# Where the softmax weights of a banded attention are masked: one mask on VectorE and a difference on GpSimd, or GpSimd and TensorE for early tiles and VectorE alone for late ones

## The chip, the cores and the metric

The kernel runs on one core of a Trainium2 chip. The metric is the device time of one execution in microseconds (us). The kernel before was run four times: 921.56, 920.98, 919.06 and 921.23 us, a median of 921.1 us. Five engines work side by side, each through its own instructions in order: TensorE (PE, with its weight loads as PEld), VectorE (DVE), ScalarE (ACT), GpSimd (POOL) and SyncE (SP), which issues most DMAs. They wait for one another through semaphores.

## The reference, cut to what matters

A batch of four sequences, `x` of shape (4, 1024, 128), goes through four residual blocks: `x + attention(layernorm(x))`, `x + ffn(layernorm(x))`, `x + mamba(layernorm(x))`, and the ffn again. The change lies in the attention alone:

```python
sliding = causal & (cols >= rows - WINDOW + 1)        # WINDOW = 32
strided = causal & ((rows - cols) % STRIDE == 0)      # STRIDE = 64
scores = jnp.where(sliding | strided, einsum('bhqd,bhkd->bhqk', Q, K) * HEAD_DIM ** -0.5, -jnp.inf)
out = einsum('bhqk,bhkd->bhqd', softmax(scores), V)   # 16 heads of 8
```

So a query sees the last 32 positions, itself among them, and every 64th position before it.

## The kernel before, in words

**Tiles.** The attention (lines 201 to 590) works on 32 tiles of 128 queries. A tile is 64 positions of two sequences at once (`bp` is the pair of sequences, `m` the tile's place among the 16 of its pair). I call tiles 0 to 15, of the first pair, pass 0, and tiles 16 to 31 pass 1. In a tile the 128 queries are four groups of 32. The window of a query reaches over two such groups, its own and the one before, and the two parts never meet: for each place k from 0 to 31 in a group a query at place q takes the own group's key if k <= q, and the key of the group before if k > q. So the kernel holds one matrix of 32 scores for each query and head, in which `copy_predicated` (lines 395 to 404) chooses by `prev_mask` between the two. The strided part, `m` more scores for each head, comes from elementwise products (`prod`, line 386) on GpSimd, which VectorE sums.

**Steps of one tile.** `scores`: TensorE (PSUM tile `ps`), ScalarE copies into `S` (line 379). `product`: GpSimd makes `prod`, 128 x 128m elements. `scores_before`: VectorE's `copy_predicated`. `softmax_scores`: VectorE sums `prod`, takes the maximum `mx` and subtracts it. `softmax_exp`: ScalarE makes `E`. `strided_products`: GpSimd makes `prodv` of `E` and the strided values, 128 x 128m elements; `strided`: VectorE sums it into `or`. `weights`: TensorE turns `E`'s 512 window weights over (PSUM tile `pt`, keys on the partitions). Then the weights are parted, which is what the change touches (lines 462 to 475): `weights_own` (VectorE) multiplies `pt` by the mask `own_t` into `eo`; `weights_all` (ScalarE) copies `pt` into `ep`; `weights_before` (GpSimd) subtracts, `ep = ep - eo`. `values` (lines 486 to 512): TensorE adds up in the PSUM tile `pa` the strided sums, 16 products of `eo` with the own group's values, and 16 (8 for m = 0) of `ep` with the values of the group before; four of these small matmuls stand side by side on the array. `divide`: VectorE divides by the sum of weights (`rden`, `o`). `turn_out`, `keep_out`, `project_out`, `residual`: TensorE turns `o` over, ScalarE keeps it (`oT`), TensorE multiplies by `woT` (`py`), VectorE adds to `x`.

**What sets the order.** The loop of lines 546 to 590 writes the order out by hand. Each engine call goes through `InOrder` (lines 49 to 62, hence L57 for nearly every instruction of the profile), which keeps it in the order of the program on its engine. In one turn i the steps belong to different tiles: GpSimd has `prodv(i-1)`, `prod(i+1)`, then the subtraction for tile i-2; VectorE `copy_predicated(i)`, `divide(i-4)`, `strided(i-2)`, the mask for i-2, `residual(i-5)`, the softmax of i; ScalarE the copy `ep(i-2)`, the copy `S(i+1)`, the exponential `E(i)`, and after it `oT(i-4)` and the copies that belong to projections of later tiles (`prep_steps`, lines 274 to 348) and `vb`; TensorE the turn of E(i-2), `py(i-5)`, `scores(i+1)`, projections, `turn_out(i-4)` and `values(i-3)`. Layer norm statistics of the ffn (`st_fa`, `mv_fa`, `rs_fa`) are put between these by the scheduler.

**Buffers.** `prod` and `prodv` share three buffers, so that `prod(i+1)` waits until VectorE has read `prodv(i-2)`. `eo`, `ep` and `kT` have two each. `kT` holds keys of four tiles on their way, by 16 DMAs, into the tile `kx`.

**What follows.** The ffn and the Mamba block (a scan over time, lines 1059 to 1154), interleaved by pieces with due times (lines 1157 to 1207), take the rest of the span. Their first instructions wait until the attention's buffers are given back.

Of the kernel before, what the change touches and what calls it, by code (L numbers as in the profile page):

```python
# [16 lines left out]
F32 = mybir.dt.float32  # L17
# [4 lines left out]
AF = mybir.ActivationFunctionType  # L22
ALU = mybir.AluOpType
# [3 lines left out]
P = 128  # L27
# [5 lines left out]
W = 32  # L33
# [6 lines left out]
CH = 512  # L40
# [3 lines left out]
def hybrid_kernel(ctx: ExitStack, tc: tile.TileContext, x, Wq, Wk, Wv, Wo, ln_g, ln_b, W_in, conv_w,  # L44
# [17 lines left out]
    ve, te, sc, gp = (InOrder(e) for e in (nc.vector, nc.tensor, nc.scalar, nc.gpsimd))  # L62
# [19 lines left out]
    for bp in range(NP):  # L82
        t = xpool.tile([P, NT, C], F32, tag=f"x{bp}", name=f"x{bp}")
# [13 lines left out]
    own_t = const.tile([P, W], F32, name="own_t")  # L97
    prev_t = const.tile([P, W], F32, name="prev_t")
# [102 lines left out]
    def attention(actx):  # L201
# [5 lines left out]
        ap2 = actx.enter_context(tc.tile_pool(name="att2", bufs=2))  # L207
# [3 lines left out]
        tiles = [(bp, m) for bp in range(NP) for m in range(NT)]  # L211
# [9 lines left out]
        VQ = W + 4  # L221
# [52 lines left out]
        def prep_steps(cc):  # L274

            bp, c = divmod(cc, NT // 4)
            yield
            xn = ap2.tile([P, 4, C], F32, name=f"xn{cc}", tag="xn")
            rs = norms.pop(cc)
            for i in range(4):  # L280
                sc.activation(
                    xn[:, i, :], xs[bp][:, 4 * c + i, :], AF.Identity, bias=rs[:, 1, i : i + 1],
                    scale=rs[:, 0, i : i + 1],
                )
            yield
            tp = spare(f"tp{cc}")
            for i in range(4):
                te.transpose(tp[:, i * P : (i + 1) * P], xn[:, i, :], ident)
            yield
            xnT = ap2.tile([P, CH], F32, name=f"xnT{cc}", tag="xnT")  # L290
            sc.copy(xnT, tp)
            yield
            pq, pk = spare(f"pq{cc}"), spare(f"pk{cc}")
            te.matmul(pk, wqkv[:, 1, :], xnT, start=True, stop=True)
            te.matmul(pq, wqkv[:, 0, :], xnT, start=True, stop=True)

            def project(i):
                pn = spare(f"pn{cc}_{i}")
                te.matmul(
                    pn[:, : 3 * C], xnT[:, i * P : (i + 1) * P], wqkv.rearrange("p i c -> p (i c)"),  # L300
                    start=True, stop=True,
                )
                return pn

            qs = ap2.tile([P, 4, C], F32, name=f"qs{cc}", tag="qs")

            def keep_rows(i, pn):
                m = 4 * c + i
                sc.copy(qs[:, i], pn[:, :C])
                sc.copy(kv[bp][:, m], pn[:, C : 3 * C])  # L310
                sc.copy(vS[bp][:, :, m], pn[:, 2 * C : 3 * C])

            yield
            kx = kxs[cc % 2]
            qT = ap2.tile([P, CH], F32, name=f"qT{cc}", tag="qT")
            if cc == 0:

                sc.copy(qT, pq)
                for t in range(4):
                    ve.tensor_tensor(  # L320
                        kx[:, t], pk[:, t * P : (t + 1) * P].unsqueeze(1).to_broadcast([P, HB, P]),
                        head_of.unsqueeze(2).to_broadcast([P, HB, P]), ALU.mult,
                    )
            else:
                kT = ap2.tile([P, CH], F32, name=f"kT{cc}", tag="kT")
                sc.copy(kT, pk)
                queues = (nc.sync, nc.gpsimd) if cc == 1 else (nc.sync,)
                for h in range(H):
                    rows = slice(h * HD, (h + 1) * HD)
                    queues[h % len(queues)].dma_start(  # L330
                        kx[rows, :, h % HB, :], kT[rows, :].rearrange("p (t x) -> p t x", t=4)
                    )
                sc.copy(qT, pq)
            prep[cc] = qT, kx
            for i0 in (0, 2):
                yield
                pn = project(i0), project(i0 + 1)
                yield
                keep_rows(i0, pn[0])
                keep_rows(i0 + 1, pn[1])  # L340
            vd = dram.tile([4, P, C], F32, name=f"vd{cc}")
            nc.sync.dma_start(vd.rearrange("t p c -> p t c"), kv[bp][:, 4 * c : 4 * c + 4, C:])
            vr = ap2.tile([P, 16, C], F32, name=f"vr{cc}", tag="vr")
            for a in range(4):
                nc.sync.dma_start(
                    vr[a * W : (a + 1) * W], vd.rearrange("t (g k) c -> k (t g) c", k=W)
                )
            prep[cc] = qT, kx, qs, vr


        S, E, prods, prodv, ew, psum, outs = ({} for _ in range(7))
# [103 lines left out]
        def weights(i):  # L455
# [3 lines left out]
            for j in range(4):  # L459
                te.transpose(pt[:, j * P : (j + 1) * P], e[:, j * P : (j + 1) * P], ident)  # L460

        def weights_own(i):
            eo = ap2.tile([P, 16, W], F32, name=f"eo{i}", tag="eo")
            pt3 = psum["t", i].rearrange("p (a q) -> p a q", q=W)
            ve.tensor_tensor(eo, pt3, own_t.unsqueeze(1).to_broadcast([P, 16, W]), ALU.mult)
            ep = ap2.tile([P, 16, W], F32, name=f"ep{i}", tag="ep")
            ew[i] = eo, ep

        def weights_all(i):
            sc.copy(ew[i][1].rearrange("p a q -> p (a q)"), psum.pop(("t", i)))  # L470

        def weights_before(i):

            eo, ep = ew[i]
            gp.tensor_sub(ep, ep, eo)

        def spread_values(cc, heads):
            vr = prep[cc][3]
# [7 lines left out]
        def values(i):  # L486

            bp, m = tiles[i]
            eo, ep = (t.rearrange("p (j g) q -> p j g q", g=4) for t in ew.pop(i))

            def value(g, j):
                k, g = divmod(4 * i + g, 16)
                return vbs[k % 2][:, g, j]

            pa = spare(f"pa{i}")[:, : 4 * VQ]
            psum["a", i] = pa.rearrange("p (j c) -> p j c", j=4)
            te.matmul(
                pa, ident, outs.pop(i).rearrange("p j c -> p (j c)"), start=True, stop=False, skip_group_check=True
            )
            for j in range(4):  # L500
                for g in range(4):
                    te.matmul(
                        pa[g * W : (g + 1) * W, j * VQ : (j + 1) * VQ], eo[:, j, g], value(g, j),
                        start=False, stop=False, skip_group_check=True,
                    )
            for j in range(4):
                for g in range(4):
                    if g % 2 or m:
                        te.matmul(
                            pa[g * W : (g + 1) * W, j * VQ : (j + 1) * VQ], ep[:, j, g], value(g - 1 if g % 2 else g - 3, j),  # L510
                            start=False, stop=j == 3, skip_group_check=True,
                        )
        def divide(i):
            pa = psum.pop(("a", i))
            rden = small.tile([P, 4, 4], F32, name=f"rden{i}", tag="rden", bufs=2)
# [30 lines left out]
        for i in range(-LEAD, last + 5):  # L546
            def at(k, stage):
                if 0 <= i + k < last:
                    stage(i + k)

            if i == -LEAD:
                weights_in()
            if i == 0:
                load_mlp()
            at(-1, strided_products)
            at(1, product)
            at(-2, weights)
            at(0, scores_before)
            at(-4, divide)
            at(-2, strided)  # L560
            at(-2, weights_own)
            at(-2, weights_all)
            at(-2, weights_before)
            at(-5, project_out)
            at(-5, residual)
            if i == 3 - LEAD:
                scores(0)
                keep_scores(0)
            if i >= 0:
                at(1, scores)  # L570
                at(1, keep_scores)
            at(0, softmax_scores)
            at(0, softmax_exp)
            if i in starts:
                preps.append(prep_steps(starts[i]))
            for p in preps:
                next(p, None)
            at(-4, turn_out)
            at(-3, values)
            at(-4, keep_out)  # L580
            for p in preps:
                next(p, None)
            cc, step = divmod(i + LEAD, 4)
            if cc + 2 < last // 4:
                stats(cc + 2, range(step, step + 1))
                if step == 3:
                    scales(cc + 2)
            cc, step = divmod(i + 1, 4)
            if 0 <= cc < last // 4:
                spread_values(cc, range(step, step + 1))  # L590
# [714 lines left out]
```

## Time and profile before

| what | us |
|---|---|
| median of four runs | 921.1 |
| the profiled execution | 921.56 |
| its span, first to last instruction | 919.8 |
| first DVE instruction of turn 5 | 46.35 |
| of turn 16 (first of pass 1) | 127.34 |
| of turn 31 | 221.69 |
| last DVE addition into x of the attention ends | 246.09 |
| busy in the span: PE, DVE, POOL, ACT | 756.4, 756.6, 746.6, 593.0 |
| DVE mask `eo`, one of 32 | 0.68 |
| ACT copy `ep`, one of 32 | 0.59 |
| POOL subtraction `ep`, one of 32 | 1.28 |

How it is read: all times are of one execution, counted from its first instruction. "Busy" is the time in which an engine executes; a matmul's end is modelled. Instructions of one engine overlap a little: where two stand back to back, the second starts some 0.08 us (DVE) before the first is shown to end, so a step on DVE is taken from start to start. The profile names tiles without their numbers; which turn a row belongs to follows from its size (`prod` of tile m has 128m elements for each partition).

### The profile page before, as it was taken

The numbers are of one execution on the slowest core, as the hardware profiler recorded it, in microseconds if no ns is written. First come the engines' busy times: TensorE is split into PE (matmuls) and PEld (weight loads), VectorE is DVE, ScalarE is ACT, GpSimd is POOL, SyncE is SP. The second block draws the span as 40 slices with busy tenths as digits, with TensorE's granted clock in tenths as the row PEclk, the third lists the DMA queues.
The fourth block names the chain that finished last, engine by engine and source line by source line (L and its number), as shares of the span: only waits on it lengthen the run. The fifth ranks groups of instructions, "written<-read, shape, count | busy, mean of one in ns | idle before, by whom it ended". The sixth has DMA issues, their size and how long they took to land.

```text
span 919.8 us, 15260 instructions
## 1 busy us (share of the span) xinstructions
PE 756.4 (82%) x5642; PEld 454.2 (49%) x5642; DVE 756.6 (82%) x1014; ACT 593.0 (64%) x1299; POOL 746.6 (81%) x580
## 2 busy tenths in 40 slices
PE   5897678865797979797789878979989889788897
PEld 2454345543476534442356434425455446455567
DVE  6799898999633278989699978897999999999862
ACT  4776447743445487789856777887777865654523
POOL 6799996999523189899988988999989999989730
PEclk9899869996599979897999997977999899899899
DMA  5633213330100111112111111212122211122001
GB/s 133 121 72 68 57 22 68 73 65 2 42 7 1 47 61 56 46 69 71 51 66 68 47 69 48 68 48 68 51 80 66 81 70 61 66 81 80 24 1 35
DMA packets 47162, 53.09 MB, mean 58 GB/s; under 512 B 4824, under 2 KB 38400, under 8 KB 47088
## 3 DMA queue, kind: packets, MB, share of 16 engines
q1 hardware_dynamic: 45920, 51.59, 19.7%
q8 instruction: 44, 0.72, 0.3%
q0 software_dynamic: 608, 0.27, 0.2%
q10 hardware_dynamic: 560, 0.26, 0.1%
q14 instruction: 30, 0.25, 0.1%
HBM read 45.82 MB, written 4.46 MB: 55 GB/s over the span
## 4 chain that ended last, share of the span: by engine, by line
DVE 22%; PE 21%; POOL 11%; ACT 9%; issue 5%; DVEq 0%; POOLq 0%; ACTq 0%
DVE hs L57 14%; POOL db L57 5%; DVE hc L57 5%; PE pys L57 4%; PE pga L57 3%; POOL hc L57 3%; PE pc L57 3%; ACT da L57 3%; ACT L57 2%; PE pgb L57 2%; PE pgc L57 1%; POOL rs_z L57 1%; ACT waste L57 1%; PE pd L57 1%; PE pfob L57 1%
## 5 line engine op out<-in xcount | busy, mean ns | idle before, releaser
L57 POOL TENSOR_TENSOR db<-du,bs 128x1024 f32<-128x1024 f32 x128 | 302.7, 2366 | 0.9 <-DMA bs<-bd 0.9
L57 ACT ACTIVATE da<-dt,a_t 128x512 f32<-128x512 f32 x256 | 175.9, 689 | 126.6 <-DVE hs L57 126.1
L57 POOL TENSOR_TENSOR hc<-hc,hc 128x512 f32<-128x512 f32 x128 | 163.1, 1275 | 44.4 <-DVE hc L57 44.2
L57 DVE TENSOR_TENSOR hc<-hs,pcc 128x1024 f32<-128x1024 f32 x128 | 156.0, 1219 | 30.2 <-PE pcc L57 22.5
L57 DVE TENSOR_TENSOR_SCAN hs<-da,db 128x512 f32<-128x512 f32 x128 | 149.3, 1206 | 15.9 <-ACT da L57 15.7
L57 DVE TENSOR_TENSOR_SCAN hs<-da,carry,db 128x512 f32<-128x512 f32 x128 | 157.0, 1267 | 4.5 <-ACT da L57 4.5
L57 PE MATMUL pys<-hc,ident 128*128 128x512 f32 x256 | 147.1, 661 | 0.8 <-POOL hc L57 0.8
L57 PE MATMUL pcc<-bc,spread 96*128 96x512 bf16 x128 | 52.3, 408 | 35.8 <-DVE hc L57 34.9
L57 PE MATMUL pga<-h1a,w 128*128 128x512 f32 x256 | 76.8, 452 | 3.8 <-ACT gate L57 1.8
L57 PEld LDWEIGHTS pys<-hc,ident 128*128 128x128 f32 x256 | 51.3, 210 | 51.6 <-issue 32.1
L57 POOL TENSOR_TENSOR prodv<-vS,E 128x128 f32<-128x128 f32 (+14 forms) x30 | 69.4, 2315 | 5.5 <-ACT E L57 5.3
L57 POOL TENSOR_TENSOR prod<-kv,qs 128x128 f32<-128x128 f32 (+14 forms) x30 | 71.1, 2370 | 1.5 <-DVE or L57 1.4
L57 PEld LDWEIGHTS pga<-h1a,w 128*128 128x128 f32 x256 | 52.9, 210 | 29.9 <-issue 7.9
L57 PE MATMUL pc<-mxnT,w_conv 128*128 128x512 f32 x128 | 61.8, 609 | 5.9 <-ACT gate L57 5.9
L57 ACT ACT_TABLE_LOAD x48 | 61.6, 1283 | 3.5 <-issue 2.6
L57 PE MATMUL pgb<-h1b,w 128*128 128x512 f32 x192 | 59.0, 453 | 4.4 <-DVE fxnTc L57 3.1
L57 ACT ACTIVATE E<-S 128x512 f32<-128x512 f32 (+15 forms) x62 | 26.5, 474 | 52.2 <-DVE S L57 52.0
L57 PEld LDWEIGHTS pgb<-h1b,w 128*128 128x128 f32 x192 | 38.2, 200 | 26.6 <-issue 7.4
L57 PE MATMUL ps<-kx,qT 64*32 64x256 f32 x1008 | 46.0, 434 | 6.2 <-DVE S L57 5.3
L57 PE MATMUL py<-woT,oT 128*128 128x128 f32 x64 | 18.0, 368 | 39.7 <-ACT oT L57 38.4
L57 POOL TENSOR_TENSOR ep<-ep,eo 128x512 f32<-128x512 f32 x32 | 41.0, 1281 | 10.0 <-ACT ep L57 8.7
L57 ACT COPY ep<-pt 128x512 f32<-128x512 f32 x32 | 18.8, 587 | 38.4 <-DVE eo L57 35.8
(223 smaller groups left out, 1551.5 us busy)
## 6 DMA issues: line engine op xcount, KB each, us to landing
bs<-bd SPq DMA_DIRECT2D x64, 512.0 KB
vr<-vd SPq DMA_DIRECT2D x32, 256.0 KB
vd<-kv SPq DMA_DIRECT2D x8, 256.0 KB
x<-in_L_attn_a_x_dram SPq DMA_DIRECT2D x15, 128.0 KB
kx<-kT SPq DMA_DIRECT2D x104, 16.0 KB
out_dram<-x SPq DMA_DIRECT2D x12, 128.0 KB
taps<-in_L_attn_b_conv_w_dram SPq DMA_DIRECT2D x1, 512.0 KB
k1s<-in_L_ffn_k_dram SPq DMA_DIRECT2D x1, 256.0 KB
```

The source lines that it names most:

```text
L57: ins = getattr(self.engine, name)(*args, **kwargs)
```

## The change

Tiles with m >= 12 are "late", four in each pass; the other 24 are early.

For an early tile VectorE does nothing here any more. ScalarE copies `pt` into `ep` as before, and `ep` stays as it is: all weights. GpSimd makes `eo` by multiplying `ep` by `own_t`. One turn later ScalarE makes a new tile `el = -eo`. `values` adds 16 (8) matmuls for `el` beside those for `ep`: the sums over the group before are those of all weights less those of the own ones. For a late tile VectorE multiplies `pt` by `own_t` into `eo` and by `prev_t` into `ep`; ScalarE and GpSimd do nothing. `el` has one buffer, and `kT` has one in place of two.

```diff
-                kT = ap2.tile([P, CH], F32, name=f"kT{cc}", tag="kT")
+                kT = ap2.tile([P, CH], F32, name=f"kT{cc}", tag="kT", bufs=1)
...
+        def late_tile(i):
+            return tiles[i][1] >= 12
+
+        def masked(engine, dst, src, mask):
+            engine.tensor_tensor(dst, src, mask.unsqueeze(1).to_broadcast([P, 16, W]), ALU.mult)
+
         def weights_own(i):
-            eo = ap2.tile([P, 16, W], F32, name=f"eo{i}", tag="eo")
-            pt3 = psum["t", i].rearrange("p (a q) -> p a q", q=W)
-            ve.tensor_tensor(eo, pt3, own_t.unsqueeze(1).to_broadcast([P, 16, W]), ALU.mult)
-            ep = ap2.tile([P, 16, W], F32, name=f"ep{i}", tag="ep")
-            ew[i] = eo, ep
+            ew[i] = [ap2.tile([P, 16, W], F32, name=f"{n}{i}", tag=n) for n in ("eo", "ep")]
+            if late_tile(i):
+                pt3 = psum.pop(("t", i)).rearrange("p (a q) -> p a q", q=W)
+                masked(ve, ew[i][0], pt3, own_t)
+                masked(ve, ew[i][1], pt3, prev_t)
 
         def weights_all(i):
-            sc.copy(ew[i][1].rearrange("p a q -> p (a q)"), psum.pop(("t", i)))
-
-        def weights_before(i):
-            eo, ep = ew[i]
-            gp.tensor_sub(ep, ep, eo)
+            if not late_tile(i):
+                sc.copy(ew[i][1].rearrange("p a q -> p (a q)"), psum.pop(("t", i)))
+
+        def weights_apart(i):
+            if not late_tile(i):
+                masked(gp, *ew[i], own_t)
+
+        def weights_less(i):
+            if not late_tile(i):
+                less = ap2.tile([P, 16, W], F32, name=f"el{i}", tag="el", bufs=1)
+                sc.activation(less, ew[i][0], AF.Copy, scale=-1.0)
+                ew[i].append(less)
...
-            eo, ep = (t.rearrange("p (j g) q -> p j g q", g=4) for t in ew.pop(i))
+            eo, *before = (t.rearrange("p (j g) q -> p j g q", g=4) for t in ew.pop(i))
...
-            for j in range(4):
-                for g in range(4):
-                    if g % 2 or m:
-                        te.matmul(... ep[:, j, g], value(g - 1 if g % 2 else g - 3, j) ...)
+            for e in before:
+                for j in range(4):
+                    for g in range(4):
+                        if g % 2 or m:
+                            te.matmul(... e[:, j, g], value(g - 1 if g % 2 else g - 3, j) ...)
...
             at(-2, strided)
+            at(-3, weights_less)
             at(-2, weights_own)
             at(-2, weights_all)
-            at(-2, weights_before)
+            at(-2, weights_apart)
```

In the built program the order of all other instructions is the same on all five engines, in the attention and behind it.

More of the change, by code (lines that the diff above doesn't have):

```diff
@@ L505, in values @@
                     )
-            for j in range(4):
-                for g in range(4):
-                    if g % 2 or m:
[L509 to L512, printed above, removed]
+            for e in before:
+                for j in range(4):
+                    for g in range(4):
+                        if g % 2 or m:
+                            te.matmul(
+                                pa[g * W : (g + 1) * W, j * VQ : (j + 1) * VQ], e[:, j, g],
+                                value(g - 1 if g % 2 else g - 3, j), start=False, stop=j == 3, skip_group_check=True,
+                            )
         def divide(i):
```

## The prediction

> **What bounds the kernel now.** I first looked at the page's busy lines: DVE and PE 82%, POOL 81%, no engine alone. The change touches the attention only, so I asked for the engines' busy time in its stretches (the columns: stretch, its length, busy us of PE, PEld, DVE, ACT and POOL with counts, granted PE clock, DMA):
>
> ```profile
> 46.35:69.51 23.16, 20.56 (x442) 13.12 (x440) 22.89 (x58) 16.20 (x44) 21.75 (x16) 1.00 0.37 72
> 69.51:105.55 36.04, 27.33 (x545) 17.49 (x545) 35.70 (x72) 20.54 (x56) 35.07 (x27) 0.91 0.25 51
> 105.55:135.93 30.38, 19.00 (x251) 11.13 (x251) 25.25 (x45) 12.46 (x32) 28.93 (x14) 0.68 0.26 49
> 135.93:163.19 27.26, 24.86 (x579) 16.30 (x581) 23.87 (x58) 19.72 (x54) 19.95 (x28) 0.98 0.31 62
> 163.19:226.40 63.21, 44.27 (x1039) 29.38 (x1028) 61.22 (x98) 33.60 (x84) 62.30 (x28) 0.89 0.25 49
> 226.40:246.10 19.70, 11.90 (x252) 9.20 (x252) 13.19 (x22) 3.42 (x10) 12.91 (x8) 0.59 0.01 2
> ```
>
> Turns 5 to 8 (first row) are paced by DVE: 22.89 of 23.16. From turn 9 on DVE and POOL are both full, and in 105.55:135.93 POOL alone (28.93 of 30.38, DVE 25.25). The timeline says which of two full engines decides. GpSimd, at the start of its unbroken run:
>
> ```profile
> 61.99 1.29 POOL L57 TENSOR_TENSOR ep<-ep,eo 128x512 f32<-128x512 f32 x1
> 63.85 2.07 POOL L57 TENSOR_TENSOR prodv<-vS,E 128x896 f32<-128x896 f32 x1 [0.57 <-ACT E L57]
> 65.89 2.64 POOL L57 TENSOR_TENSOR prod<-kv,qs 128x1152 f32<-128x1152 f32 x1
> 68.48 1.27 POOL L57 TENSOR_TENSOR ep<-ep,eo 128x512 f32<-128x512 f32 x1
> ```
>
> and VectorE where it has caught up with GpSimd:
>
> ```profile
> 109.90 1.75 DVE L57 TENSOR_REDUCE or<-prodv 128x128 f32<-128x1536 f32 x1 [3.16 <-POOL prodv L57]
> ...
> 113.83 2.02 DVE L57 TENSOR_REDUCE S<-prod 128x224 f32<-128x1792 f32 x1 [1.13 <-POOL prod L57]
> ...
> 122.83 2.16 DVE L57 TENSOR_REDUCE S<-prod 128x240 f32<-128x1920 f32 x1 [0.60 <-POOL prod L57]
> ```
>
> The bracket is the idle time before the row and who ended it. After 63.85 GpSimd waits for nobody until 133.5; in pass 1, from 165 on, it idles 0.5 us before 168.41 and 0.24 before 175.38, then never until 237.9. GpSimd's work grows by some 0.55 us a tile (two products of 128m elements), VectorE's by 0.33, so every pass turns from VectorE's into GpSimd's. A third row matters at the end, ScalarE's copy and GpSimd's subtraction behind VectorE's mask:
>
> ```profile
> 239.89 0.59 ACT L57 COPY ep<-pt 128x512 f32<-128x512 f32 x1 [4.65 <-DVE eo L57]
> ```
>
> ```profile
> 236.64 1.30 POOL L57 TENSOR_TENSOR ep<-ep,eo 128x512 f32<-128x512 f32 x1
> 240.56 1.27 POOL L57 TENSOR_TENSOR ep<-ep,eo 128x512 f32<-128x512 f32 x1 [2.62 <-ACT ep L57]
> ```
>
> **Prices.** VectorE's mask shows 0.68 us, but the next instruction starts 0.59 to 0.60 later (65.39 to 65.98): I take 0.6, taken from 24 tiles and added to 8. GpSimd's subtraction is 1.28. A GpSimd multiply by a repeated mask isn't in the trace. The rows of its size are prod 128x512 at 1.28, prodv 128x512 at 1.07, and prodv 128x640 at 1.68, which is 1.34 for 512. I take 1.28, since in prod too one operand is repeated over the outer dimension; 1.07 and 1.34 are kept for the range. So early tiles change nothing on GpSimd, late ones free it of 1.28 each. ScalarE's el is nearest to E 128x512 (0.63, SBUF to SBUF) and the copy ep (0.59); queued back to back such copies start 0.48 apart: 0.5, within 0.48 to 0.63. TensorE's 16 more matmuls: ep's follow eo's by 0.29 (62.26 to 62.55), 0.49 at half clock; 24 times 0.3 is 7 us on an engine with 3 us and more idle per 20.
>
> el could force ScalarE to change function tables. The trace shows no table load from 25 to 247, although Identity, Exp and plain copies alternate there; a scaled Copy activation isn't among them. The Trainium skill, "ScalarE: Activation LUTs", section on table sets, says that cheap functions like copy lie in every set, so no load would come. If loads came all the same, two of 1.28 (the profile's ACT_TABLE_LOAD row, mean 1283 ns) for each of 24 tiles would put 62 us on ScalarE; since Identity and plain copies need none beside Exp, I leave this out of the cases.
>
> kT with one buffer costs nothing: the projection that feeds the next kT stands on TensorE behind the scores that wait for all of the former kT's DMAs.
>
> **The sum, in order of time** (turn i starts with copy_predicated of tile i).
>
> 1. *Turns 2 to 8.* Up to turn 4 ScalarE paces (it is full), and el only replaces its waits: 0. Then VectorE gains 0.6 a turn. But GpSimd idles only 0.28 (before 56.47), 0.15 (57.90) and 0.57 (63.85) there, and 0.52 before 46.52, of which I count 0.2; so its front comes forward by 1.2 us at most; its next work, prodv of tile 7, would start at 62.65 instead of 63.85. Gain 1.2; VectorE's other savings turn into waits for prod.
> 2. *Turns 9 to 13.* GpSimd paces, same work: 0.
> 3. *Turns 14 to 17.* GpSimd loses 4 x 1.28, VectorE gets 4 x 0.6. prod of tile 14 is still 1.2 early. From there VectorE, no longer waiting (its 0.60 before 122.83 goes), paces with 9.1 us a turn: turn 16 starts 1.1 early, turn 18 only 0.7. So late tiles give back 0.5 here.
> 4. *Turns 17 to 22.* Around 142.8 to 148.4 ScalarE is the limit (5.42 busy of 5.62; VectorE waits 1.68 for its copy S). In turn 17 it has no ep to copy, in turn 18 no el yet: the 0.7 stays. From turn 19 VectorE gains 0.6 a turn, ScalarE pays 0.5, and turn 21, with 5.50 busy of 5.67, gives some of it back. I get E of tile 22 and its prodv 1.0 early.
> 5. *Turns 23 to 31.* GpSimd's last idle (0.24) goes too: 1.25. Then it paces up to prod of tile 31, now ending at 226.37: 0 more.
> 6. *Tail.* The two subtractions at 226.37 and 231.38 are gone. prodv of tile 30 follows at once (225.1); that of tile 31 has to wait for its E, whose softmax starts at prod's end: 225.1 + 4.2 to the last subtraction + 0.9 for E = 230.2, ends 234.35 instead of 236.7. VectorE then sums it (2.4) and masks twice (1.2): 237.95. Before, the last weights were ready at 241.83 (mask to 239.8, copy to 240.5, subtraction); now TensorE is bound by po of tile 30 at 238.8, one turn of matmuls before the last rden: 240.9 against 243.38. Gain of the attention's end: 2.5.
>
> Behind it all instructions keep their order and wait for the attention's buffers, so 2.5 us should go through. The profiled execution took 921.56, 1.76 more than its span: 921.56 - 2.5 = 919.1. It was the slowest of four runs, 0.46 above their median; on the median of 921.1 this is **918.6 us**.
>
> The rest is not perfectly rigid: the granted clock is 0.59 in 226.40:246.10, and the four runs spread over 2.5 us. The Trainium skill, "TensorE: Matmul & The Clock Gate", in "What's actually happening", says the gate follows activity in free-running windows of about 3.4 us. By that page a shift of 2.5 us may land the ffn's first matmuls in another window, an estimate of up to 1.7 us either way.
>
> **Rivals.**
>
> *A cheaper mask.* With GpSimd at 1.07, the 13 masks in its paced stretches (tiles 6 to 11 and 21 to 27) save another 2.7: 915.9. Only one size of prodv speaks for it. At 1.34 they cost 0.8: 919.4.
>
> *The gain is given back.* VectorE's second mask falls in four turns where it is nearly as full as GpSimd (in 163.19:226.40 it is 61.22 of 63.21). If steps 1 and 4 bring nothing, because ScalarE delays E just as much, only the tail's 1.2 is left: 919.9. If VectorE, and not GpSimd, paces turns 30 and 31, 2 x 0.6 take that too: 921.1. For: ScalarE's full turns; against: VectorE waits 0.70 for prod of tile 31 before.
>
> *ScalarE becomes the bound, and it is slower.* el stands in its queue ahead of ep, S and E, and waits for GpSimd. S is what VectorE's next turn starts with, E what GpSimd's does. From turn 18 to 22 there are five such turns near ScalarE's limit. If each pays a whole 0.6, pass 1 is 3.0 late less the 0.7 brought: 2.3, and the tail returns 1.2: 922.2. It decides from the point at which GpSimd's mask ends less than el, ep and S (0.5 + 0.5 + 0.6) before the softmax's end. In turn 12: prod, then mask 1.28 and these 1.6 are 2.9 against 3.8 from prod to the end of the subtraction; so 0.9 is left there, about 0.4 at turn 8. Against it: the copy ep no longer waits for VectorE's mask (35.8 us in 20 waits), so ScalarE starts earlier.
>
> **How the numbers follow.** My sum, -1 to -4, 0.54; cheaper mask or more gained in VectorE's turns 0.17; given back 0.16; ScalarE 0.13. I call 0.2%, 1.84 us, what a measurement here can tell from no change, so faster means below 919.26. Of the first case I count 0.43 there and 0.11 within; of the second all; of the third 0.02 faster, 0.14 within; of the fourth 0.03 within, 0.10 slower. Faster 0.62, same 0.28, slower 0.10. The range goes from the cheap mask, 915.9, less a little spread, to the edge of ScalarE's case: 915.5 to 921.9.
>
> **What would show it.** Right: GpSimd's masks at 1.28 and prodv of tile 7 (128x896) near 62.7; VectorE waiting for prod in turns 10 to 13; GpSimd idle and VectorE full in turns 15 to 17; prod of tile 31 ending about 225.1; the last x of the attention near 243.6. Wrong: el waiting long for GpSimd with VectorE waiting for S; masks beyond 1.34; table loads before 243; or an early end of the attention that isn't there at 290.

## The result, and the profile after

The changed kernel takes 921.7 us (median of 45 runs, 918.3 to 924.7), the kernel before 920.0 us beside it (71 runs, 917.9 to 924.1). The ratio is 1.0014, 95% interval 1.0005 to 1.0022: 1.3 us slower, give or take 0.8, where 2.5 us faster was predicted. The profiled execution of the changed kernel took 918.81 us (span 916.7), less than its median; of its 45 runs 22 took over 921.9 us, of before's 71 only 12.

One pair of profiles would mislead here, so I compare stretches over several. Turn 1 starts anywhere from 29.1 to 32.9 us, whichever kernel runs; all lengths are therefore counted from it. "Tail" is the time from the start of prod of tile 31 to the end of the last addition into `x`. The three other profiles of before, and the second and third of after, belong to experiments below.

| stretch, us | before: its profile; three others | predicted change | after: its profile; second; attention alone |
|---|---|---|---|
| turn 1 to 14 | 75.84; 75.92 to 75.99 | -1.2 | 75.15; 76.99; 75.13 |
| turn 14 to 18 | 37.23; 36.34 to 36.43 | +0.5 | 37.62; 37.68; 37.63 |
| turn 18 to 23 | 26.08; 26.03 to 26.06 | -0.3 | 26.57; 28.03; 26.81 |
| turn 23 to prod of tile 31 | 53.31; 53.32 to 53.40 | -0.25 | 52.97; 53.02; 52.98 |
| tail | 23.92; 23.41 to 23.47 | -1.25 | 22.78; 22.86; 22.80 |
| turn 1 to the attention's end | 216.38; 215.10 to 215.24 | -2.5 | 215.09; 218.58; 215.35 |

The stretches of after, cut at the starts of turns 5, 9, 14, 17 and 22, at the end of prod of tile 31, and at the end (columns as in the table of stretches of before: length, then busy us of PE, PEld, DVE, ACT, POOL, then clock and DMA):

```profile
46.02:68.51 22.49, 21.55 (x660) 15.01 (x653) 20.97 (x53) 18.24 (x48) 21.68 (x17) 1.00 0.38 74
68.51:104.77 36.26, 28.82 (x727) 18.57 (x714) 33.07 (x66) 23.14 (x61) 35.29 (x27) 0.95 0.26 52
104.77:135.78 31.01, 20.77 (x351) 12.45 (x351) 26.99 (x49) 11.46 (x30) 25.45 (x11) 0.67 0.25 49
135.78:162.79 27.01, 23.35 (x512) 15.24 (x510) 22.21 (x54) 21.03 (x56) 18.25 (x26) 1.00 0.31 62
162.79:226.16 63.37, 48.40 (x1423) 34.37 (x1422) 58.25 (x92) 36.99 (x91) 62.57 (x28) 0.89 0.24 50
226.16:244.71 18.55, 10.01 (x216) 7.94 (x216) 14.19 (x24) 2.44 (x8) 7.97 (x4) 0.68 0.01 2
```

Each engine lost or won the work that was counted: VectorE's 58.25 in the fifth row stands against 61.22, GpSimd's 25.45 in the third and 7.97 in the last against 28.93 and 12.91. But the third row is longer (31.01 against 30.38).

GpSimd, where step 1 put its gain (its timeline in after):

```profile
61.91 1.31 POOL L57 TENSOR_TENSOR eo<-ep,own_t 128x512 f32<-128x512 f32 x1
63.16 2.08 POOL L57 TENSOR_TENSOR prodv<-vS,E 128x896 f32<-128x896 f32 x1
65.18 2.65 POOL L57 TENSOR_TENSOR prod<-kv,qs 128x1152 f32<-128x1152 f32 x1
```

The mask costs what the subtraction did, and the idle 0.57 before prodv of tile 7 is gone. But this prodv came forward by only 0.6 to 0.8 us, not 1.2: counted from turn 1 it starts at 33.5 us in the profiles of the change with an undisturbed turn 4, and at 34.1 to 34.3 in four of before. One wait for ScalarE is left, and longer than the 0.28 of before: the mask waits for the copy `ep`, which now stands behind `el` in a ScalarE that is busy from 50.98 on (timelines of after, GpSimd, then ScalarE):

```profile
56.58 1.28 POOL L57 TENSOR_TENSOR eo<-ep,own_t 128x512 f32<-128x512 f32 x1 [0.50 <-ACT ep L57]
```

```profile
55.40 0.64 ACT L57 ACTIVATE el<-eo 128x512 f32<-128x512 f32 x1
55.94 0.57 ACT L57 COPY ep<-pt 128x512 f32<-128x512 f32 x1
```

VectorE still waits for GpSimd afterwards (its timeline, turns 12 and 13 of after):

```profile
100.60 1.89 DVE L57 TENSOR_REDUCE S<-prod 128x208 f32<-128x1664 f32 x1 [0.79 <-POOL prod L57]
109.17 1.75 DVE L57 TENSOR_REDUCE or<-prodv 128x128 f32<-128x1536 f32 x1 [3.20 <-POOL prodv L57]
113.10 2.02 DVE L57 TENSOR_REDUCE S<-prod 128x224 f32<-128x1792 f32 x1 [0.52 <-POOL prod L57]
```

In turns 15 to 17 VectorE shows no wait at all, so both masks of a late tile lengthen the turn. These are tiles 14 and 15:

```profile
132.58 0.68 DVE L57 TENSOR_TENSOR eo<-pt,own_t 128x512 f32<-128x512 f32 x1
133.18 0.68 DVE L57 TENSOR_TENSOR ep<-pt,prev_t 128x512 f32<-128x512 f32 x1
...
139.26 0.68 DVE L57 TENSOR_TENSOR eo<-pt,own_t 128x512 f32<-128x512 f32 x1
139.85 0.68 DVE L57 TENSOR_TENSOR ep<-pt,prev_t 128x512 f32<-128x512 f32 x1
```

Then comes what the prediction did not see. All waits of VectorE from turn 19 to the start of turn 23, in after:

```profile
148.06 0.78 DVE L57 COPY_PREDICATED S<-prev_mask,ps 128x512 f32<-128x512 int32 x1 [1.81 <-ACT S L57]
154.26 0.26 DVE L57 RECIPROCAL rden<-pa 128x16 f32<-128x16 f32 x1 [1.58 <-PE pa L57]
159.17 0.26 DVE L57 RECIPROCAL rden<-pa 128x16 f32<-128x16 f32 x1 [0.73 <-PE pa L57]
164.09 0.26 DVE L57 RECIPROCAL rden<-pa 128x16 f32<-128x16 f32 x1 [0.48 <-PE pa L57]
168.96 0.79 DVE L57 COPY_PREDICATED S<-prev_mask,ps 128x512 f32<-128x512 int32 x1 [0.85 <-ACT S L57]
```

and the same turns in a second profile of the kernel before:

```profile
149.67 0.79 DVE L57 COPY_PREDICATED S<-prev_mask,ps 128x512 f32<-128x512 int32 x1 [1.68 <-ACT S L57]
155.60 0.26 DVE L57 RECIPROCAL rden<-pa 128x16 f32<-128x16 f32 x1 [0.77 <-PE pa L57]
170.11 0.78 DVE L57 COPY_PREDICATED S<-prev_mask,ps 128x512 f32<-128x512 int32 x1 [0.40 <-ACT S L57]
```

VectorE's saved 0.6 a turn turned into waits for `pa`, the sums that TensorE makes: 2.79 us in three turns instead of 0.77 in one. TensorE itself has no idle time left there. These are all its waits from the start of turn 19 to just behind that of turn 23, first in the second profile of before, then in after:

```profile
150.62 0.49 PE L57 MATMUL py<-woT,oT 128*128 128x128 f32 x2 [0.72 <-ACT oT L57]
165.57 0.49 PE L57 MATMUL py<-woT,oT 128*128 128x128 f32 x2 [0.19 <-ACT oT L57]
171.12 0.49 PE L57 MATMUL py<-woT,oT 128*128 128x128 f32 x2 [0.77 <-ACT oT L57]
```

```profile
149.02 0.49 PE L57 MATMUL py<-woT,oT 128*128 128x128 f32 x2 [0.71 <-ACT oT L57]
169.84 0.49 PE L57 MATMUL py<-woT,oT 128*128 128x128 f32 x2 [0.78 <-ACT oT L57]
```

The end of the attention is as planned, GpSimd idle before its last prodv and VectorE waiting for TensorE (two timelines of after):

```profile
226.16 3.82 POOL L57 TENSOR_TENSOR prodv<-vS,E 128x1792 f32<-128x1792 f32 x1
231.37 4.06 POOL L57 TENSOR_TENSOR prodv<-vS,E 128x1920 f32<-128x1920 f32 x1 [1.40 <-ACT E L57]
```

```profile
242.00 0.26 DVE L57 RECIPROCAL rden<-pa 128x16 f32<-128x16 f32 x1 [2.00 <-PE pa L57]
...
244.42 0.29 DVE L57 TENSOR_TENSOR x<-x,py 128x128 f32<-128x128 f32 x1 [1.43 <-PE py L57]
```

### The profile page after: what moved, and what is told of

It reads as the page before. It is cut to its first block, busy times and chain, and to the rows that moved or that the text cites. A ratio compares the mean times of both kernels' runs of the same rounds, so it can differ in the third digit from the quotient of the medians.

```text
span 916.7 us, 16743 instructions
## 1 busy us (share of the span) xinstructions
PE 760.8 (83%) x6378; PEld 460.7 (50%) x6378; DVE 748.6 (82%) x998; ACT 601.3 (66%) x1315; POOL 736.6 (80%) x572
## 4 chain that ended last, share of the span: by engine, by line
DVE 30%; PE 28%; POOL 19%; ACT 14%; issue 8%; DMA 1%; DVEq 0%; SPq 0%; POOLq 0%; ACTq 0%
DVE hs L57 14%; POOL prod L57 5%; PE pga L57 5%; DVE hc L57 5%; PE pys L57 4%; PE pc L57 4%; POOL db L57 4%; POOL prodv L57 3%; ACT da L57 3%; DVE S L57 3%; ACT L57 3%; POOL hc L57 2%; PE pgb L57 2%; POOL eo L57 2%; PE pfoa L57 2%
## 5 line engine op out<-in xcount | busy, mean ns | idle before, releaser
L57 PE MATMUL pga<-h1a,w 128*128 128x512 f32 x256 | 74.6, 443 | 2.5 <-ACT gate L57 1.8
L57 PEld LDWEIGHTS pc<-mxnT,w_conv 128*128 128x128 f32 x128 | 24.6, 194 | 36.9 <-issue 26.8
L57 POOL TENSOR_TENSOR du<-dt,u 128x512 f32<-128x512 f32 x16 | 20.4, 1281 | 26.5 <-ACT dt L57 26.5
L57 DVE TENSOR_REDUCE S<-prod 128x16 f32<-128x128 f32 (+14 forms) x30 | 36.5, 1215 | 5.8 <-POOL prod L57 5.7
```

What stands on the lines that cost most here:

```text
L57: ins = getattr(self.engine, name)(*args, **kwargs)
```

## The experiments

My theory after the result: *TensorE* (the matmuls of `el` are on the path where TensorE is full) together with *VectorE* (the late tiles' second masks give the gain back). Rivals: ScalarE's copy `el`; and that the attention does end earlier, but the stage behind it does not follow, because its length depends on where the clock's windows fall (stretches in which TensorE's granted clock is recorded as half). In the texts below, theory A is that `el`'s work fills TensorE or ScalarE, B is *VectorE*, and C is this last rival.

### Leaving out the matmuls of el, or the copy

`no_el_matmuls` makes `el` and does not multiply by it, so the part of the group before is the sum over all weights:

```diff
-            for e in before:
+            for e in before[:1]:
```

> The changed kernel without the matmuls that add el (early tiles' sums then lack the part of the own weights); el is still made on ScalarE. Theory A with TensorE as the part that binds: last prod 0.8 to 1.2 earlier than the changed kernel's 221.9, end near 243.6. Theory A with ScalarE as the part that binds: unchanged within 0.3.

`no_el_copy` makes no `el` and multiplies `eo` in its place, so own weights are added and not subtracted:

```diff
-            at(-3, weights_less)
...
-            eo, *before = (...)
+            eo, ep = (...)
+            before = [ep] if late_tile(i) else [ep, eo]
```

> The changed kernel without el on ScalarE: the 16 more matmuls are kept, but take eo (the own weights are then added and not taken away). Theory A with ScalarE binding: last prod 0.8 to 1.2 earlier than the changed kernel's 221.9, end near 243.6. With TensorE binding: unchanged within 0.3.

Measured: `no_el_matmuls` 919.44 us, ratio to before 0.9975 (0.9962 to 0.9989); `no_el_copy` 921.21, ratio 0.9996 (0.9980 to 1.0012). Turn 18 to 23 took 25.81 us without the matmuls, 0.25 less than before, as step 4 had it; without the copy 27.78. So the matmuls alone are worth 3.6 us (1.0014 less 0.9975, of 920; give or take some 1.5), more than the whole difference. In the profiles the attention from turn 1 is 2.2 us shorter without them (212.87 against 215.09). The copy by itself is not what fills turns 18 to 23; from 1.0014 to 0.9996 the intervals overlap. In pass 0 the copy does count: without it prodv of tile 7 starts 33.1 us after turn 1 and without the matmuls 32.9 (33.2 in `att_no_el_matmuls` below), against 33.5 with both and 34.2 before. So leaving out either one brings 1.0 to 1.3 us, about the 1.2 of step 1.

### The two halves in the whole kernel

`early_only` leaves the late tiles as before, `late_only` the early ones.

> Only the early half of the change: early tiles as in the changed kernel, late ones as before (VectorE own mask, ScalarE copy, GpSimd subtraction). Theory A (el fills TensorE and ScalarE in turns 18 to 23, where VectorE's saving is lost): GpSimd's last prod starts within 0.3 us of before (222.2) and the attention ends within 0.4 of 246.1. Theory B (VectorE's late masks give back what the early tiles won): without them the early gain of 1.2 is there in full, last prod near 221.0, end near 244.9. Theory C (the stage behind the attention runs in steps of the clock's windows): whatever the end, the total is 918 to 924 and does not follow it.

> Only the late half: early tiles as before, late ones by two VectorE masks. Theory A: no el anywhere, so turns 18 to 23 are as before, last prod within 0.3 us of 222.2, and the tail alone brings the end to 244.7 to 245.0. Theory B: VectorE with two masks paces turns 14 to 17 and 30 to 31, last prod 0.5 or more later than before and the end at 245.5 or later. Theory C: the total 918 to 924, not following the end.

Measured: 919.92 us, ratio 0.9984 (0.9964 to 1.0004), and 922.99, ratio 1.0012 (0.9993 to 1.0031). The halves point to opposite sides, neither certain by itself. The attention of `early_only` ended at 246.02 us, as theory A expected; that of `late_only` at 246.91, as theory B expected. But the profile of `late_only` also lost 1.6 us between turns 4 and 5 (7.07 us instead of 5.4 to 5.7), which has nothing to do with late tiles; so I went on without the stage behind and with more than one profile.

### The attention alone

These kernels end behind the attention; what follows is left out and `x` is written out. The order on every engine up to there is that of the whole kernel.

```diff
+    for bp in range(NP):
+        ...
+                nc.sync.dma_start(out[2 * bp + b2]..., xs[bp]...)
+    return
     fw = ctx.enter_context(tc.tile_pool(name="ffnw", bufs=1))
```

> The kernel before, cut off behind the attention: its own order on all engines up to there, with the first ffn statistics, and then x written out; ffn and Mamba are left out. It is the base for the three others; some 262 to 270 us. Theory C says that the spread of its runs is small (under 2 us), since the spread comes from the stages behind; if its runs spread over 4 us and more, the attention itself varies.

> The changed kernel, cut off in the same way. Theory A (early tiles lose on TensorE what they win on VectorE): 1.0 to 1.8 us under att_before in the median, as in the one profiled pair (1.4). Theory C then has to explain that the whole kernel is no faster. The rival, that the profiled pair was a lucky one: 0 to 1 us slower than att_before, as the whole kernel's 45 runs.

> att_after without the el matmuls (the own weights are not taken away in early tiles; el is still made). Theory A, TensorE: 1.5 to 2.5 us under att_after. If TensorE's matmuls cost nothing, as predicted: within 0.4 of att_after.

Measured (medians of 4, 4 and 5 runs): 253.67, 253.46 and 251.18 us. Within the spread of these few runs the change makes the attention neither longer nor shorter, so the 1.0 to 1.8 us less of theory A are not there; the rival's 0 to 1 us more are not ruled out. Without `el`'s matmuls the attention is 2.3 us shorter than with them, as expected, and 2.5 us shorter than before; the whole kernel without them was 2.3 us below before.

Then the halves, against `att_before_2`, the attention of before on their chip:

> The attention alone of the kernel before, a second time: the base for the two cut kernels that run beside it. It leaves out everything behind the attention and writes x out. Every theory: as the first time, 253.7 us within 0.7, and 23.5 us from the start of prod of tile 31 to the last addition into x.

> The attention alone, leaving out what follows it: early tiles as after the change, late tiles as before. Theory TensorE with theory VectorE: about 1.0 to 1.7 early from turn 10 to turn 20, given back at turns 20 to 23 by el's matmuls, so that prod of tile 31 is within 0.7 of att_before_2 counted from turn 1, and the tail is as long as there (23.4): within 0.7 us of att_before_2 in all. Prediction: 1.2 early up to prod of tile 31 and to the end.

> The attention alone, leaving out what follows it: early tiles as before, late tiles by VectorE's two masks. Theory VectorE: turns 14 to 18 lose 0.5 to 1.5 us against att_before_2, the tail gives 0.7 to 1.0 back: within 0.7 of it in all. Prediction: 0.5 lost in turns 14 to 17 and 1.2 won in the tail.

The medians (252.02, 252.82 and 252.84 us; four runs each, spread over 3.0 to 3.7 us) tell nothing apart; the stretches do:

| us, less att_before_2 | turn 1 to 14 | 14 to 18 | 18 to 23 | 23 to prod 31 | tail | all |
|---|---|---|---|---|---|---|
| att_early_only | -0.80 | +0.09 | +0.49 | -0.42 | -0.19 | -0.83 |
| att_late_only | +0.07 | +1.13 | +0.07 | -0.04 | -0.18 | +1.05 |
| att_after | -0.79 | +1.29 | +0.78 | -0.39 | -0.64 | +0.25 |

The halves add up to the whole (+0.22 against +0.25), in part by luck: from turn 18 to 23 they make 0.56 where the whole has 0.78, and in the tail, the least steady term, -0.37 against -0.64. Two expectations were missed: the tail of `att_late_only` gave 0.2 us and not 0.7 to 1.0, so that it is 1.05 above in all, and `att_early_only` is 0.83 below, not within 0.7. The late tiles cost 1.1 us in turns 14 to 18, nearly twice a second mask of 0.6. Those of tiles 12 and 13 were free, since VectorE waits for GpSimd there; those of tiles 14 and 15 were paid whole. In the timeline of `att_late_only` they stand in a VectorE without waits, before the starts of turns 17 and 18:

```profile
133.34 0.68 DVE L57 TENSOR_TENSOR ep<-pt,prev_t 128x512 f32<-128x512 f32 x1
...
135.94 0.73 DVE L57 COPY_PREDICATED S<-prev_mask,ps 128x512 f32<-128x512 int32 x1
...
140.01 0.68 DVE L57 TENSOR_TENSOR ep<-pt,prev_t 128x512 f32<-128x512 f32 x1
...
142.56 0.76 DVE L57 COPY_PREDICATED S<-prev_mask,ps 128x512 f32<-128x512 int32 x1
```

### The kernel before with more matmuls

The cleanest test of TensorE: before, with the 16 (8) matmuls of `ep` done twice for every early tile. No other engine gets other work. The part of the group before is added twice.

```diff
-            for j in range(4):
+            for j in [0, 1, 2, 3] * (2 if m < 12 else 1):
                 for g in range(4):
                     if g % 2 or m:
```

> The attention alone of the kernel before, in which TensorE does the 16 (8) matmuls of ep twice for every early tile, as many more as the change adds; nothing else is changed, so VectorE, ScalarE and GpSimd have the work of before. It adds the part of the group before twice, and it leaves out what follows the attention. Theory TensorE (its matmuls are on the path in turns 17 to 23, where it has no idle time): 1.5 to 3 us above att_before_2, lost between turn 17 and turn 23, with rden waiting for pa there. Theory of the prediction (TensorE's idle time covers them) and theory VectorE (only the second masks of the late tiles give the gain back): within 0.5 of att_before_2.

> The whole kernel before, with ep's 16 (8) matmuls done twice for every early tile (the part of the group before is added twice); nothing else differs. The attention alone grew by 2.0 us by its profile and 2.8 by its medians. If the end of the attention goes through to the end of the kernel: ratio 1.002 to 1.003, 2 to 3 us above before. If the stage behind it absorbs shifts (its clock windows decide): 0.999 to 1.001.

Measured: 254.81 us against 252.02 for `att_before_2` (medians); from turn 1 to the end 217.53 against 215.10, 2.4 us more, in two places: 0.54 in turns 1 to 14 (0.38 of it from turn 4 to 5) and 1.26 from turn 18 to 23; the tail adds 0.46. VectorE's waits there, in `att_more_matmuls`:

```profile
156.41 0.26 DVE L57 RECIPROCAL rden<-pa 128x16 f32<-128x16 f32 x1 [1.03 <-PE pa L57]
162.02 0.26 DVE L57 RECIPROCAL rden<-pa 128x16 f32<-128x16 f32 x1 [0.82 <-PE pa L57]
171.90 0.79 DVE L57 COPY_PREDICATED S<-prev_mask,ps 128x512 f32<-128x512 int32 x1 [0.21 <-ACT S L57]
```

and in `att_before_2`, all between 153 and 165 us:

```profile
155.05 0.26 DVE L57 RECIPROCAL rden<-pa 128x16 f32<-128x16 f32 x1 [0.78 <-PE pa L57]
```

(The text on `more_matmuls` says 2.0 us by the profile; counted from turn 1 it is 2.4.) So the prediction's cost of nothing is refuted by TensorE's work alone. Over the twenty profiles of this study the stretch from turn 18 to 23 sorts the kernels without exception: 25.81 to 26.10 us in the twelve of kernels that do no more matmuls for these tiles than before, 26.52 to 28.03 in the eight of those that do (mean 27.31: 1.3 more than before, 0.25 a turn, about what 16 matmuls take back to back: the step of `values` lasts 1.31 us instead of 1.04 where nothing interrupts it). Not all of the range is the matmuls' own time. `early_only` and `att_early_only` run the same order in these turns, but take 27.62 and 26.51 us; 0.9 of it lies in the scores' matmuls (`ps`, 6.9 us from start to start against 6.0), and the profile shows no cause. The whole kernel `more_matmuls` had a ratio of 1.0018 (0.9997 to 1.0038): just below the expected 1.002 to 1.003, and no change is within the interval. In its profile the attention took 218.05 us, 2.8 more than in the second profile of before, and the stage behind it 669.4, 2.7 less.

### Only the parts that paid

`att_tail` is before with two VectorE masks for tiles 30 and 31 alone.

> att_before with the two VectorE masks in tiles 30 and 31 alone, everything else as before (kT with one buffer). If the tail's gain is what step 6 says: 1.0 to 1.6 us under att_before, as much as or more than att_after. If VectorE paces turns 32 and 33: within 0.4 of att_before.

Measured: 253.77 us (5 runs), as `att_before`: the expected 1.0 to 1.6 us less are not there. Its profile has a tail of 22.99, 0.45 shorter, and a turn 4 longer by 1.6.

`mixed` takes the early scheme for tiles 4 to 9, the late one for tiles 28 to 31, and leaves all others as before:

```diff
         def late_tile(i):
-            return tiles[i][1] >= 12
+            return i >= 28
+
+        def early_tile(i):
+            return 4 <= i < 10
...
```

> The attention alone, leaving out what follows it, with each half of the change only where it paid: in pass 0 tiles 4 to 9 by GpSimd's mask, el and the 16 more matmuls; in pass 1 tiles 28 to 31 by VectorE's two masks; all other tiles as before. Theory TensorE with theory VectorE: turn 14 is 1.0 to 1.2 early and this stays up to turn 27, since neither the matmuls of turns 17 to 23 nor the second masks of turns 14 to 17 are there; the tail gives 0.7 to 1.0 more: 1.7 to 2.3 us below att_before_2. If the gain of pass 0 is lost for another reason (ScalarE's or TensorE's full turns 18 to 23 absorb any earlier start): only the tail's 0.7 to 1.0.

> The whole kernel with each half of the change only where it paid: tiles 4 to 9 by GpSimd's mask, el and 16 more matmuls, tiles 28 to 31 by VectorE's two masks, all others as before. If the end of the attention goes through: 1.7 to 2.3 us below the kernel before, ratio 0.9975 to 0.9982. If the stage behind the attention doesn't follow its end (clock windows), the ratio lies within 0.999 to 1.001 while att_mixed is shorter.

> mixed once more, since its 12 runs spread from 914.8 to 924.4: tiles 4 to 9 by GpSimd's mask and 16 more matmuls, tiles 28 to 31 by VectorE's two masks, all others as before. Its attention alone was 1.4 us shorter by the profile. If the end goes through: ratio 0.9980 to 0.9990; if not: 0.9993 to 1.0010.

By its profile the attention alone was 1.4 us shorter from turn 1 (213.72 against 215.10), less than the 1.7 to 2.3 expected: turn 1 to 14 gives 0.7, turn 18 to 23 takes 26.03 as before, the tail gives 0.75. Its median, 251.92 us of six runs against 252.02 of `att_before_2`, does not show it. The whole kernel does not show it: ratios 0.9996 (0.9973 to 1.0019) and 1.0000 (0.9983 to 1.0017), so neither beats before. The first whole profile lost 1.5 us from turn 4 to 5 and 0.8 from turn 17 to 18; in the second the attention was 214.03, 1.1 shorter. Whether that gain is lost behind the attention or only hidden by the spread stays open.

### The two kernels once more

> The kernel before, unchanged: what is left of a difference is the measurement's. Ratio within 0.9985 to 1.0015. If the clock's windows decide the stage behind the attention, its length (span less end of the attention, 673.7 in the first profile) differs by 1 us or more in this second profile, and the attention lacks the 0.8 us that turn 17 lost in the first.

> The kernel after the change, unchanged. Theory TensorE and VectorE (the attention is 0.2 us longer, nothing else changes): ratio 0.9990 to 1.0015, attention 215.1 to 215.4 from turn 1 to its end, and a stage behind it that differs from the first profile's 672.0 as freely as that of before. If the change lengthens the stage behind the attention by itself: ratio 1.0010 to 1.0025, and that stage over 674 here.

Measured: ratios 1.0002 (0.9986 to 1.0018) and 1.0006 (0.9986 to 1.0027). The second profile of before has an attention of 215.24 us, 1.1 shorter than the first; turn 17 to 18 took 6.01 instead of 6.85, and the stage behind is 1.6 us shorter (672.0 against 673.7): both as expected if the clock's windows decide. The second profile of after took 923.48 us in all, 4.7 more than the first, and 3.5 of that are in the attention, outside the expected 215.1 to 215.4. Its TensorE timeline shows where:

```profile
41.44 1.88 PE L57 MATMUL pk<-xnT,wqkv 128*128 128x512 f32 x2
...
159.28 0.27 PE L57 MATMUL py<-woT,oT 128*128 128x128 f32 x1 [0.92 <-issue]
```

In `before_again` the first of these rows reads:

```profile
41.37 1.12 PE L57 MATMUL pk<-xnT,wqkv 128*128 128x512 f32 x2
```

The two `pk` matmuls at turn 4 took 1.88 us where they took 1.12 in `before_again`, and VectorE waited 2.28 us for `pa` (0.65 in `before_again`). A half clock is recorded from 39.6 to 43.0 us in `after_again`, across them, and from 33.7 to 40.5 in `before_again`, ahead of them. The second row's bracket is idle time for which the profile has no cause, inside the stretch where TensorE is full. The stage behind the attention took as long as before: 671.8 (span less the attention's end) and 672.0 in the two profiles of after, 672.0 and 673.7 in those of before. So the rival that the change lengthens the stage behind finds no support. It is not excluded for a lengthening of about 1 us: over the eleven whole profiles of this study that stage took 669.4 to 677.4 us.

## Why the prediction was wrong

*TensorE's matmuls: the step that failed.* They were "7 us on an engine with 3 us and more idle per 20", cost 0. The price of 0.3 a tile was right (0.27 back to back); that idle time covers it was wrong. Idle time per 20 us is an average. From about 149 to 169 us TensorE has next to none (busy 19.06 of 20.00 us in before, 19.87 in after), and the sign was in a row that the prediction itself showed: in 135.93:163.19 PE is busy 24.86 of 27.26 us, more than VectorE's 23.87. I named ScalarE as the limit there and read no timeline of TensorE. With them turn 18 to 23 takes 0.5 to 2.0 us more than before, without them 0.2 less; what makes the upper part of that range stays open. In turns 1 to 14 they cost 0.35 to 0.6 (75.13 against 74.78, 75.15 against 74.53 without them).

*Step 1* (-1.2): GpSimd's front came forward by 0.7 us (prodv of tile 7 at 33.52 from turn 1 in `att_early_only`, 34.23 in `att_before_2`), not 1.2. The mask's price was right: 1.28 us. But the sum put `el` at nothing up to turn 4 and gave it no price in turns 5 to 8, and there the mask still waits 0.50 us for `ep` behind `el`; without `el`'s copy, or without its matmuls, the front came 1.0 to 1.3 us forward. *Step 2* (0) held: prod of tile 14 is still 0.7 early, and turn 14 starts 0.8 early.

*Step 3* (+0.5): two whole second masks were paid, those of tiles 14 and 15, 1.2 to 1.3 us against the other profiles of before. Against the profile that the sum was made from it is 0.4 (37.62 against 37.23), as predicted: that execution's turn 17 lasted 6.85 us where others have 6.01 to 6.03 (a half clock recorded from 130.2 to 137.0 us reaches into it, and the granted clock of that turn was 0.92), so part of the second masks fell into time that was lost already.

*Step 4* (0.3 more by prodv of tile 22): +0.5 to +2.0 instead, with the matmuls. The row that it gives for turn 21, 5.50 busy of 5.67, is that of turn 22 (163.19 to 168.86). *Step 5* (-0.25): -0.35 measured.

*Step 6* (tail, -1.25): the new tail was worked out as 22.7 and took 22.8. But the old one of 23.92 was long; three other profiles of the attention of before have 23.4 to 23.5 from the same start. So 0.5 us of this gain, and the 0.8 of turn 17, were an accident of the one execution the sum was made against; it cost the prediction 1.1 to 1.3 us (216.38 against 215.10 to 215.24).

*The sum.* -2.5 was predicted; with the measured terms, and the undisturbed turn 4, it is -0.8 + 1.25 - 0.35 - 0.6, and 0.5 to 2.0 for the matmuls' turns: 0.0 to +1.5. The whole kernel says +1.3 (0.5 to 2.0), so its loss lies within what the attention shows. That the matmuls eat the gain is shown; where the kernel loses the 1.3 us beyond that is not, since the attention alone has the same median with the change as without it. That the attention's end goes through is supported by `no_el_matmuls` (2.3 us below before as a whole, 2.5 in the attention alone); `more_matmuls` is undecided, and `mixed` does not show it.

*The rivals.* ScalarE as the bound had the right turns (18 to 22) and nearly the right total, but for these turns the wrong engine, so the total is luck: `el` waited 26.4 us for GpSimd in nine waits, and without it these turns are as long. In pass 0 `el` took its part of step 1's gain. "The gain is given back" was right for the late tiles. The cheaper mask was wrong, and table loads did not come: after has 48 in the span, as before, and none from 25 to 247 us, as the Trainium skill, "ScalarE: Activation LUTs", section on table sets, lets expect.

## What to carry to other kernels

Before instructions are added to an engine at no cost, read its timeline in the turn where it is fullest, one turn at a time: a mean idle share of 10% can be no idle time at all where it matters. When one engine is relieved, its saved time can become a wait for the next fullest engine, as here, so that one must not be given the work. Take the length of each stretch from several executions before a change of a fraction of a per cent is summed against one.

## What the runs showed of the hardware

- Executions of one kernel differ by more than this change: its attention took 215.09 and 218.58 us in two profiles. Part of it is the clock: in four of twenty profiles, of four kernels, turn 4 took 6.6 to 7.1 us instead of 5.4 to 5.9, with the two `pk` matmuls there at 1.88 to 2.08 us; in the sixteen others they took 1.12 or 1.13. In those four a half clock of 3.4 us is recorded across them, from 39.1 to 41.4 us on; in the sixteen it lasts 6.8 us, begins at 31.0 to 34.4 and is over before them. All recorded half clocks last 3.4 us or a multiple of it, unless the profile ends in them, and they begin at other times in each profile (31.2 and 33.7 us in two of before). The Trainium skill, "TensorE: Matmul & The Clock Gate", "What's actually happening", describes free-running windows of about 3.4 us, which agrees, and puts the cost of the clock's ramp under 1% of a typical span. The 0.9 to 1.6 us that turn 4 lost are under 0.2% here, but as much as the change; what the half clock costs over the whole span no run shows.
- TensorE's instructions show as DMA traffic. The queue of this kind grew from 44 to 50 packets with the matmuls of `el`, also in `more_matmuls` (before, then after):

```profile
q8 instruction: 44, 0.72, 0.3%
```

```profile
q8 instruction: 50, 0.82, 0.4%
```

- Idle time of TensorE of 0.15 us or more without a cause ("issue") inside the attention came in eight of the eleven profiles of kernels with some or all of the change's early part, 0.2 to 1.8 us in sum, in one of the two with `ep`'s matmuls doubled, and in none of the seven others. It lay between 65 and 69 us, between 154 and 164, or at 200.7. That TensorE then waits for instructions to be fetched is a guess that no run tests.
